# A four-layer graph network: the last row tile as quarters, layer 1's inner units kept as rows, degrees behind a conditional

## The chip, the cores and the metric

The kernel runs on one core of a Trainium2 chip. The metric is the device time of one execution in microseconds (us). Engines: PE (TensorE), DVE (VectorE), ACT (ScalarE), POOL (GpSimd) and SP (SyncE, which here only issues transfers). Every matrix product is in float32; one product in the program is two PE instructions in the trace.

## The reference

A graph of N = 2708 nodes with D = 256 features passes four layers; each adds a graph step and a feed-forward step to x. Layers 0 to 2 are touched.

```python
# layer 0, graph: msg = layernorm(x) @ W + B
#   weights = where(adj < 1, exp(-2 * (1/adj - 1)**2), 0);  x += weights @ msg
# layer 0, feed-forward: 8 experts, each row goes to its best 2
#   h = gelu(xn @ W1[e] + b1[e]);  out += w[e] * (h @ W2[e] + b2[e])
# layer 1, graph
A = adj + jnp.eye(adj.shape[0], dtype=adj.dtype)
D = 1.0 / jnp.sqrt(jnp.sum(A, axis=1))
A = A * D[:, None] * D[None, :]
support = input @ W
out = A @ support                       # relu(out + b)
# layer 1, feed-forward: one hidden layer for all experts, each row goes to its best 1
H = jax.nn.gelu(xf @ W1 + b1, approximate=False)      # 1024 units
probs = jax.nn.softmax((H @ Wg + bg) / TEMP, axis=-1)
assign = jnp.argmax(probs, axis=-1)
for e in range(Wd.shape[0]):
    y = H @ Wd[e] + bd[e]
    sel = (assign == e)[:, None]
    out = out + jnp.where(sel, probs[:, e:e + 1] * y, 0.0)
# layer 2, graph: attention with a mask adj > 0, out = (e @ h) / sum(e)
```

## The kernel before

Rows are cut into 22 tiles of 128 (NT); the last has 20 (LAST; FULL = 21 is its number). x stays in SBUF for the whole program.

**Graph steps.** The adjacency comes transposed from memory. The row tiles of the result are made in groups (GROUPS: 9, 7 and 6 tiles; GROUPS1: 8, 8 and 6; in layer 2 by fives). For a group, the loop `for j in range(NT)` takes one strip `adrow` of 128 source rows (20 in the last), turns it into weights (`weigh` in layer 0: Ln, Exp, Exp on ACT and two DVE steps; in layer 1 a mask, and the identity added on the diagonal; in layer 2 the attention weights `e`) and multiplies it into one accumulator for each tile of the group. These products are lines 739 (layer 0), 965 (layer 1) and 1159 (layer 2). At j = 21 only 20 of the 128 rows that a product can take are there. The last row tile of the result is made apart, with products by columns of 32 (`last_sums`, L256).

**Sending.** When a group is complete, `send` (layer 0) or `send1` (layer 1) normalizes its rows, computes the gate, and `route` gives each row a place in a list ordered by expert; POOL scatters the rows to that place in memory (`taken`), with the row's number and weight behind the 256 features (XW = 258). In layer 1 the gate needs the hidden units H, so `send1` computes them (`hidden`, L317), with the weights `w1`. Send1 of a group is computed among the products of the next one. In layer 0 the buffer `xr` of the last send is that of the send before, whose scatter has to land first (the DVE normalization is L182).

**Blocks.** The feed-forward steps take the list in blocks of 128 places, each with one expert. The class `Blocks` runs items of two blocks: POOL gathers the rows (`xs<-taken`, L465), PE turns them (L518), DVE copies them (L524), PE computes the units (L551) and ACT their gelu (L553), PE makes the output (L560), DVE adds the bias and weighs (L562, L563), and POOL scatters rows to `given` (L451). In layer 0 an item has two blocks of one expert; in layer 1 each block has its own expert, and L551 computes again the units that send1 has had. The first items (NA) hold full blocks of the first groups only, so they can start before the last group is routed. A fixed number (ALWAYS) of the others is always run; what may remain stands under a conditional, `run_rest`, a branch that every engine takes (L569).

**The seam to layer 1.** In the shadow of layer 0's blocks DVE adds up the adjacency's strips into `cs` (128 partial sums for each node). After the last block, but ahead of the conditional, 22 products with a column of ones give the degrees, each copied by DVE (L814, L815). Behind the conditional SP loads `both`, the two results of every row (`given`), which DVE adds to x (L869) before layer 1's normalization and projection (L195, L238; L920 scales by the inverse root of the degree, which DVE makes by Newton steps, L152 to L158).

**Order and memory.** Instructions are issued on each engine in the program's order as a scheduler at build time leaves it. SP's queue has all large loads; POOL has the gathers, the scatters and small loads. Buffers come from pools with a given number of buffers; a load waits until its buffer's last reader is done.

```python
te.matmul(p[:q, n - pair[0], :], lhsT=ad[:, k : k + q],
          rhs=sup[:r, j, :], start=(j == 0 and n == pair[0]),
          stop=(j == NT - 1 and n == pair[-1]))
```

Of the kernel before, what the change touches and what calls it, by code (L numbers as in the profile page):

```python
# [66 lines left out]
def adj_ffn4(ctx: ExitStack, tc: tile.TileContext, a: dict, out: bass.AP):  # L67
# [116 lines left out]

    def shift(st, G):

        nb = small.tile([P, G], F32, name="nb", tag=f"nb{G}", bufs=2)
        v.scalar_tensor_tensor(nb, st[0][:, :, 0], -1.0, st[1], op0=ALU.mult, op1=ALU.mult)
        return nb
# [61 lines left out]
    def last_sums(p, cols, values, n):  # L251
# [10 lines left out]
        return p[:LAST, :n]  # L262

# [210 lines left out]

    class Blocks:
# [4 lines left out]

        def __init__(self, pool, l, each, given, weights):
            self.pool, self.each, self.given = pool, each, given
            self.weights, self.ahead, self.rows, self.at = weights, [], [], [0, 0]
            self.late = None
            self.ik, self.ok = f"taken{l}", f"given{l}"

        def fetch(self, item):

            ei, b = item[0][0], item[1]
            n = 2 * P // self.each  # L490
            es = [nc.values_load(ei[0:1, i : i + 1], engines=[mybir.EngineType.SP], min_val=0,
                                 max_val=E - 1,
                                 skip_runtime_bounds_check_because="at most E - 1 by a minimum")
                  for i in range(n * b, n * b + n)]
            self.ahead.append(self.weights(self.at[0], es))
            self.at[0] += 1

        def fetch_rows(self, item):
            (_, ix, _), b, past, src, full = item
            n = 2 * P // self.each  # L500
# [7 lines left out]
            for k in range(2):  # L508
                i = ix[:, b, k : k + 1] if n == 1 else ix[:, 2 * b + k, :]
                gather(xs[:, k, :], src, i, src.shape[0] - 1, self.ik, past)  # L510
# [16 lines left out]
        def run(self, pool, items, during=None, after=None):  # L527
# [9 lines left out]
            for n in range(len(items)):  # L537
# [20 lines left out]
                for k in range(2):  # L558
                    for f in range(HC):
                        te.matmul(q[:, k, :], lhsT=hT[:, f, k * P : (k + 1) * P], rhs=w2[k][:, f, :],  # L560
                                  start=(f == 0), stop=(f == HC - 1))
                    v.tensor_tensor(y[:, k, :], q[:, k, :], w2[k][:, HC, :], ALU.add)  # L562
# [4 lines left out]
        def run_rest(self, pool, items, left, most):  # L567
# [3 lines left out]
            pin(scattered[self.ok][-1].name)  # L571

# [29 lines left out]
    taken = [tc.dram_tile([2 * N, XW], F32, name="taken0"), tc.dram_tile([N, XW], F32, name="taken1")]  # L602
# [14 lines left out]
    with ExitStack() as l0:  # L617
        hw = l0.enter_context(tc.tile_pool(name="h0", side="right", reuse_waits="tile", bufs=1))

        def weights0(b, es):  # L620
# [3 lines left out]
            i = nc.sync.dma_start(wa, a["L0_ffn_W1b"][bass.ds(es[0], 1)].rearrange("e p n -> p (e n)"))  # L624
# [4 lines left out]
            nc.sync.dma_start(wb, a["L0_ffn_W2p"][bass.ds(es[0], 1)].rearrange("e p n -> p (e n)"))  # L629
            w2 = wb.rearrange("p (f d) -> p f d", d=D)  # L630
            return wa[:, :2048].rearrange("p (c h) -> p c h", c=DC), wa[:, 2048:], (w2, w2)
# [939 lines left out]
```

## Time and profile before

| | us |
|---|---|
| median of 3 runs (lowest to highest) | 2080.28 (2075.45 to 2080.8) |
| the profiled execution | 2077.27 |
| its span, first to last instruction | 2075.3 |
| PE busy | 1974.2 (95%) |
| DVE, ACT, POOL busy | 1098.1, 661.8, 287.4 |

The mean granted clock of PE is 0.967 of full speed; 226.64 MB are moved. By the trace, layer 0's graph step ends at about 262 us, its feed-forward step at 635, the seam to layer 1 lasts to 701 (products begin inside it), layer 1's graph step ends at 982 and its feed-forward step at 1193, layer 2's graph step at about 1458 and its feed-forward step at about 1650; layer 3 takes the rest.

How to read the lines: a group gives line, engine, operation, output<-input by the program's names, shapes and count, then busy time and the mean ns of one, then the idle time of the engine just before and what ended it. Matmuls are pipelined, so their mean duration is longer than the distance from one to the next. A windows row gives the stretch and its length, each engine's busy time with its instructions, the granted clock, the busy share of the 16 DMA engines, and GB/s. A row of waits gives the total, the number and the longest. In the chain and the timeline the first number is the start and the second the length.

### The profile page before, as it was taken

Reading aid. Unit: us, or ns where it says so; the run is one execution under the profiler, and the core shown is the slowest. Engines: PE = TensorE matmul, PEld = TensorE weight load, DVE = VectorE, ACT = ScalarE, POOL = GpSimd, SP = SyncE. Lnnn points to the kernel's source line nnn. Section 1 sums busy time; section 2 is a strip of 40 time slices with the busy share of each in tenths; the row PEclk is TensorE's granted clock in tenths of the full one; section 3 lists DMA queues with packets and bytes.
Section 4 is the critical chain, followed back from the end, with each engine's and each line's share of the span. In section 5 each row is a group of like instructions: output and inputs, shape, how many; then the busy total and the mean of one; then the engine's idle time right before and its main releaser. Section 6 shows DMA issues by size and latency. Waiting matters only on the chain.

```text
span 2075.3 us, 25886 instructions
## 1 busy us (share of the span) xinstructions
PE 1974.2 (95%) x9673; PEld 1422.3 (69%) x9673; DVE 1098.1 (53%) x2513; ACT 661.8 (32%) x1449; POOL 287.4 (14%) x315
## 2 busy tenths in 40 slices
PE   7999979999996999999999979999899999999997
PEld 5888868888885888877788858888566622232334
DVE  7677742543335231334321165455355588897876
ACT  8778722222223204031422251223234410120112
POOL 1004362333320000103133110000000000000000
PEclk9999979999997999999999989999899999999999
DMA  8435557877744341524256330000101000000000
GB/s 266 140 106 147 191 192 266 334 286 295 282 147 134 110 132 43 154 54 147 88 187 210 138 94 1 1 1 1 41 1 31 16 1 21 21 26 11 16 11 24
DMA packets 80611, 226.64 MB, mean 109 GB/s; under 512 B 15218, under 2 KB 38746, under 8 KB 71264
## 3 DMA queue, kind: packets, MB, share of 16 engines
q1 hardware_dynamic: 69056, 196.17, 28.4%
q0 software_dynamic: 11424, 28.74, 4.1%
q8 instruction: 80, 1.31, 0.3%
q14 instruction: 51, 0.42, 0.1%
HBM read 206.46 MB, written 20.65 MB: 109 GB/s over the span
## 4 chain that ended last, share of the span: by engine, by line
PE 55%; DMA 5%; issue 3%; DVE 2%; ACT 2%; POOL 1%; POOLq 0%; DVEq 0%; SPq 0%; ACTq 0%
PE num L1483 11%; PE acc L965 9%; PE ps_acc L1159 9%; PE ps_tmp L317 7%; PE den L1494 6%; DMA given<-ys,xs 4%; PE ps_acc L1335 3%; PE ps_tmp L238 3%; PE ps_tmp L195 1%; PE ps_acc L238 1%; PE ps_tmp L897 1%; POOL xs L465 1%; PE ps_acc L551 1%; POOL given L451 0%; DMA mine<-given 0%
## 5 line engine op out<-in xcount | busy, mean ns | idle before, releaser
L1478 DVE SCALAR_TENSOR_TENSOR e<-arena,G,mask 128x1024 f32<-128x1024 f32 (+2 forms) x264 | 294.2, 1150 | 44.3 <-PE den L1494 43.9
L560 PE MATMUL yacc<-wb,hTs 128*128 128x256 f32 x1152 | 263.1, 381 | 0.9 <-DVE ys L562 0.7
L1483 PE MATMUL num<-e,wh 128*64 128x512 f32 (+4 forms) x1056 | 243.6, 558 | 0.0
L560 PEld LDWEIGHTS yacc<-wb,hTs 128*128 128x128 f32 x1152 | 216.4, 191 | 30.6 <-DVE ys L562 2.3
L965 PE MATMUL acc<-sup,adrow 128*128 128x256 f32 (+1 forms) x924 | 214.4, 390 | 0.0
L739 PE MATMUL acc<-msg,wt 128*128 128x256 f32 (+1 forms) x924 | 208.6, 383 | 0.0
L1159 PE MATMUL ps_acc<-hh,e 128*128 128x257 f32 (+1 forms) x924 | 207.9, 381 | 0.0
L965 PEld LDWEIGHTS acc<-sup,adrow 128*128 128x128 f32 (+1 forms) x924 | 176.7, 195 | 30.6 <-issue 5.5
L739 PEld LDWEIGHTS acc<-msg,wt 128*128 128x128 f32 (+1 forms) x924 | 174.2, 191 | 27.2 <-issue 1.8
L1159 PEld LDWEIGHTS ps_acc<-hh,e 128*128 128x128 f32 (+1 forms) x924 | 171.4, 190 | 28.6 <-issue 2.5
L551 PE MATMUL ps_acc<-xTs,wa 128*128 128x256 f32 x768 | 179.2, 386 | 6.4 <-issue 4.1
L1483 PEld LDWEIGHTS num<-e,wh 128*64 128x64 f32 (+1 forms) x1056 | 74.3, 138 | 155.2 <-issue 121.6
L553 ACT ACTIVATE hTs<-ps_acc,wa 128x256 f32<-128x256 f32 x192 | 90.6, 473 | 257.8 <-PE yacc L560 171.3
L551 PEld LDWEIGHTS ps_acc<-xTs,wa 128*128 128x128 f32 x768 | 142.1, 192 | 35.2 <-issue 4.6
L196 ACT COPY xT<-ps_tmp 128x256 f32<-128x256 f32 x120 | 40.9, 363 | 322.5 <-PE ps_tmp L195 322.2
L1494 PE MATMUL den<-e,wh 128*32 128x512 f32 (+4 forms) x1056 | 137.9, 551 | 0.0
L562 DVE TENSOR_TENSOR ys<-yacc,wb 128x256 f32<-128x256 f32 x72 | 30.5, 424 | 199.7 <-PE yacc L560 199.5
L1156 DVE SCALAR_TENSOR_TENSOR e<-Rb,G,mask 128x640 f32<-128x640 f32 (+2 forms) x110 | 85.2, 775 | 94.3 <-PE ps_acc L1159 94.3
L451 POOL DMA_INDIRECT taken<-xr,r_ix x66 | 78.1, 1183 | 359.7 <-DVE b_vec L387 190.2
L451 POOL DMA_INDIRECT given<-ys,xs x72 | 91.8, 1275 | 208.7 <-DVE ys L563 161.2
L942 DVE TENSOR_SCALAR mask<-adrow 128x1024 uint8<-128x1024 f32 (+1 forms) x66 | 41.5, 629 | 134.4 <-DMA adrow<-in_adjT 134.2
L465 POOL DMA_INDIRECT xs<-taken,b_ix x72 | 75.0, 1042 | 191.0 <-DVE xTs L524 90.6
(392 smaller groups left out, 2464.8 us busy)
## 6 DMA issues: line engine op xcount, KB each, us to landing
adhalf<-in_adjT SPq DMA_DIRECT2D x42, 677.0 KB
wb<-in_L_ffn_W2p SPq DMA_DIRECT2D x24, 1152.0 KB
wb<-in_L_ffn_Wdp SPq DMA_DIRECT2D x24, 1152.0 KB
wa<-in_L_ffn_W1b SPq DMA_DIRECT2D x24, 1028.0 KB
adrow<-in_adjT SPq DMA_DIRECT2D x42, 512.0 KB
adrow<-in_adjT SPq DMA_DIRECT2D x42, 320.0 KB
adrow<-in_adjT SPq DMA_DIRECT2D x21, 576.0 KB
adrow<-in_adjT SPq DMA_DIRECT2D x21, 448.0 KB
```

The source lines that it names most:

```text
L317: te.matmul(p[:, :w], lhsT=w1[:, c, f * P : (f + 1) * P], rhs=xnT[:, c, c0 : c0 + w], start=(c == 0), stop=(c == DC - 1))
L451: i = g.indirect_dma_start(out=dst, out_offset=bass.IndirectOffsetOnAxis(ap=ix, axis=0), in_=src, in_offset=None, bounds_check=bound, oob_ ...
L465: i = g.indirect_dma_start(out=dst, out_offset=None, in_=src, in_offset=bass.IndirectOffsetOnAxis(ap=ix, axis=0), bounds_check=bound, oob_ ...
L551: te.matmul(p[:, f % 2, :], lhsT=w1[:, c, f * P : (f + 1) * P], rhs=xT[:, c, :], start=(c == 0), stop=(c == DC - 1))
L553: s.activation(hT[:, f, :], p[:, f % 2, :], AF.Gelu, bias=bias[:, f : f + 1])
L560: te.matmul(q[:, k, :], lhsT=hT[:, f, k * P : (k + 1) * P], rhs=w2[k][:, f, :], start=(f == 0), stop=(f == HC - 1))
L739: te.matmul(p[:q, n - pair[0], :], lhsT=wt[:, k : k + q], rhs=msg[:r, j, :], start=(j == 0 and n == pair[0]), stop=(j == NT - 1 and n == p ...
L965: te.matmul(p[:q, n - pair[0], :], lhsT=ad[:, k : k + q], rhs=sup[:r, j, :], start=(j == 0 and n == pair[0]), stop=(j == NT - 1 and n == p ...
L1159: te.matmul(p[:q, : D + 1], lhsT=e[:r, k : k + q], rhs=hh[:r, j, :], start=(j == 0), stop=(j == NT - 1))
L1478: v.scalar_tensor_tensor(e[:r, :w], Rb[:r, k, :w], G[:r, j, 2 * pair + k, :], mask[:r, j, c0 : c0 + w], op0=ALU.max, op1=ALU.mult)
L1483: te.matmul(num[k * DK : (k + 1) * DK, hf, :q], lhsT=wh[:r, j, 2 * pair + k, :DK], rhs=e[:r, h0 - c0 : h0 - c0 + q], start=(j == 0), stop= ...
L1494: te.matmul(den[z : z + Q, :q], lhsT=wh[:ri, i, 2 * pair + k, DK : DK + 1].to_broadcast([ri, Q]), rhs=e[:ri, h0 - c0 : h0 - c0 + q], start ...
```

## The change

Four parts are made together.

1. *Row quarters.* At j = 21 the strip's 20 rows are loaded several times, each time at another quarter of 32 partitions, with the columns of other tiles beside them (`last_rows`; POOL sets the tile to ones first). `spread_out` copies the 20 rows of values to all four quarters. `last_product` multiplies with one quarter of the array, at its row position, and `by_turns` orders the tiles so that four in a row differ in quarter and in PSUM tile. In layer 0 this moves to j = 19 of the first group and j = 12 of the others, and the weights need a third of the columns; in layers 1 and 2 it stays last.
2. *Degrees.* The products with ones go behind the conditional, into one PSUM tile with two reads, and Ln and Exp on ACT take the place of the copies and DVE's Newton steps. The additions of `both` to x are ordered behind the last `shift`.
3. *Layer 0's last `xr`* gets a pool of its own.
4. *Layer 1's units as rows.* send1 turns its units back to rows (8 transposes a tile), DVE copies them, and POOL writes them to memory (`hid`). `taken` now has a row number and a weight only. The class `Units` runs single blocks: it gathers the names, gathers by them the rows of `hid` (128 rows of 1024), turns them (8 transposes, two ACT copies), and makes the output as before. Names have one buffer for each block, set to ones once (`MOST` of them), gathered rows three, Wd three. NA is 9 instead of 8, ALWAYS 15 instead of 16. The first names and rows are gathered at j = 17 of the last group, the first Wd after its last product.

```diff
+    def spread_out(values):
+        n = values.shape[1]
+        p = ps_tmp()
+        for z in range(0, P, Q):
+            te.matmul(p[z : z + Q, :n], lhsT=ident[:LAST, :Q], rhs=values[:LAST, :], start=True,
+                      stop=True, tile_position=(0, z))
+        s.copy(values, p[:, :n])
+    def last_rows(dst, parts):
+        g.memset(dst, 1.0)
+        for q, k, c0, w in parts:
+            nc.sync.dma_start(dst[q * Q : q * Q + LAST, k : k + w],
+                              a["adjT"][FULL * P :, c0 : c0 + w])
+    def last_product(p, q, weights, k, values, stop=True):
+        te.matmul(p, lhsT=weights[q * Q : q * Q + LAST, k : k + P],
+                  rhs=values[q * Q : q * Q + LAST, : p.shape[1]], start=False, stop=stop,
+                  tile_position=(q * Q, 0))
+    def by_turns(own):
+        return [(n, t, k) for z in range(2) for n, (t, k, _) in enumerate(own) if n % 2 == z]
...
+    class Units(Blocks):
+            self.names = pool.tile([P, MOST, 2], F32, name="names")
+            g.memset(self.names, 1.0)
+            self.hs = pool.tile([P, 3, HC * P], F32, name="hs")
+            g.memset(self.hs, 0.0)
...
+        def turn(self, pool, h):
+            hT = pool.tile([P, HC, P], F32, name="hTs", bufs=3)
+            for f in range(0, HC, 4):
+                p = ps_acc()
+                for i in range(4):
+                    te.transpose(p[:, i * P : (i + 1) * P], h[:, (f + i) * P : (f + i + 1) * P], ident)
+                s.copy(hT[:, f : f + 4, :], p.rearrange("p (f t) -> p f t", f=4))
+            return hT
...
+        def more(self, weights=True):
+            while self.names_todo and len(self.named) + len(self.rows) < 4:
+                self.fetch_names(self.names_todo.pop(0))
+            while self.rows_todo and len(self.rows) < 3:
+                self.fetch_rows()
+                self.rows_todo -= 1
+            while weights and self.todo and len(self.ahead) < 2:
+                self.fetch(self.todo.pop(0))
...
+                y = pool.tile([P, D], F32, name="ys", bufs=2)
+                q = pools["psum"].tile([P, W], F32, name="yacc", bufs=2)[:, :D]
+                for f in range(HC):
+                    te.matmul(q, lhsT=hT[:, f, :], rhs=w2[:, f, :], start=(f == 0), stop=(f == HC - 1))
+                v.tensor_tensor(y, q, w2[:, HC, :], ALU.add)
+                v.tensor_scalar(y, y, m[:, 1:2], None, op0=ALU.mult)
+                scatter(self.given, m[:, 0:1].bitcast(I32), y, self.given.shape[0] - 1, self.ok)
...
+            xr = (tp if len(parts) == 1 else own_rows[0]).tile(
+                [P, GMAX if len(parts) == 1 else G, 2, XW], F32, name="xr", bufs=1)[:, :G]
...
         work0.run_rest(hc, more, left[0], ALWAYS)
-        for t in range(NT):
-            r = rows(t)
+        for q, t0, t1 in ((P, 0, FULL), (LAST, FULL, NT)):
             d = ps_tmp()
-            te.matmul(d[:r, :1], lhsT=cs[:, t * P : t * P + r], rhs=ones, start=True, stop=True)
-            v.tensor_copy(deg[:r, t : t + 1], d[:r, :1])
+            for t in range(t0, t1):
+                i = te.matmul(d[:q, t : t + 1], lhsT=cs[:, t * P : t * P + q], rhs=ones,
+                              start=(t == t0), stop=(t == t1 - 1))
...
+            lnexp(deg[:q, t0:t1], d[:q, t0:t1], AF.Ln, bias=ones[:q])
+        lnexp(deg, deg, AF.Exp, scale=-0.5)
...
-        v.tensor_scalar(deg, deg, 1.0, None, op0=ALU.add)
-        deg = rsqrt(tp, deg, NT)
...
+                for i, k, r in own:
+                    t, h = tiles[i], gt.tile([P, HC * P], F32, name="hrow", bufs=2)
+                    for f in range(0, HC, 4):
+                        p = ps_tmp()
+                        for z in range(4):
+                            te.transpose(p[:r, z * P : (z + 1) * P], hT[:, f + z, k : k + r], ident)
+                        v.tensor_copy(h[:r, f * P : (f + 4) * P], p[:r, :])
+                    g.dma_start(hid[t * P : t * P + r, :], h[:r])
...
+                if j < FULL:
+                    nc.sync.dma_start(ad, a["adjT"][j * P : j * P + r, c0 : c0 + w])
+                else:
+                    last_rows(ad, [(q, 0, c0, w) for q in range(P // Q)])
...
+                if end and j == NT - 5:
+                    past = list(scattered["taken1"])
+                    work1.begin([(full, b, past, taken[1][:held], True) for b in range(NA)])
```

## The prediction

> **What bounds the kernel now.** I read the page's shares first, then the stages as windows, then the groups that the change touches, kept apart by shape, then the waits of PE, the chain, and POOL's timeline at the end of layer 1's last group.
>
> ```profile
> span 2075.3 us, 25886 instructions
> PE 1974.2 (95%) x9673; PEld 1422.3 (69%) x9673; DVE 1098.1 (53%) x2513; ACT 661.8 (32%) x1449; POOL 287.4 (14%) x315
> ...
> core 0: us, PE busy (x) PEld busy (x) DVE busy (x) ACT busy (x) POOL busy (x), PEclk, DMA share, GB/s
> 0.00:262.00 262.00, 245.34 (x1194) 210.10 (x1194) 197.37 (x441) 200.63 (x243) 58.49 (x72) 0.99 0.56 173
> 635.00:701.00 66.00, 46.14 (x216) 35.94 (x216) 35.79 (x137) 29.51 (x78) 2.93 (x5) 0.82 0.42 134
> 701.00:988.00 287.00, 281.28 (x1414) 235.47 (x1414) 96.85 (x296) 46.59 (x97) 26.84 (x26) 0.97 0.38 112
> 988.00:1193.00 205.00, 202.22 (x994) 169.21 (x994) 43.18 (x137) 62.51 (x133) 46.46 (x47) 0.99 0.45 153
> ```
>
> PE is the bound: 95% of the span, 98% of layer 1's products (701 to 988) and 99% of its feed-forward stage (988 to 1193). So TensorE work taken out there counts in full until something else fills the stage, and DMA, at 153 GB/s, is the next resource. Only the seam of 635 to 701 is loose: PE 70%.
>
> ```profile
> L551 PE MATMUL ps_acc<-xTs,L_ffn_W 128*128 128x256 f32 x384 | 91.5, 388 | 7.3 <-DVE xTs L524 7.3
> L518 PE MATMUL turned<-ident,xs 128*128 128x128 f32 x144 | 23.4, 282 | 0.4 <-DVE xTs L524 0.4
> L524 DVE COPY xTs<-turned 128x512 f32<-128x512 f32 x36 | 23.5, 654 | 46.7 <-PE turned L518 46.7
> L965 PE MATMUL acc<-sup,adrow 20*128 20x256 f32 x42 | 11.4, 425 | 0.0
> L1494 PE MATMUL den<-e,wh 128*32 128x512 f32 x672 | 91.3, 600 | 0.0
> L256 PE MATMUL acc<-msg,wt x44: 374/379/403, 209.7 to 212.6; 128*32 128x256 f32 x42, 20*32 20x256 f32 x2
> ```
>
> Busy times overlap, so I price by pitch. On the chain 32 instructions of 256 columns take 6.94 us, and 16 take 3.47: 0.217 each, and a product is two. Four 128x128 transposes take 0.43: 0.108 each. L965's 42 instructions on 20 rows are the last row tile of one layer: 42 x 0.217 = 9.1 us for 20 rows of 128.
>
> ```profile
> PE ps_tmp L195 <- ACT xn L207: 13.2, 1, 13.2
> PE ps_acc L551 <- DVE xTs L524: 7.3, 4, 5.5
> PE ps_acc L195 <- DVE xr L182: 6.6, 1, 6.6
> ...
> 644.40 2.23 issue
> 647.22 6.15 DMA both<-given
> ...
> 967.64 1.04 POOL L465 DMA_INDIRECT xs<-taken,b_ix  x1 [3.99 <-DMA adrow<-in_adjT]
> 982.53 1.51 POOL L465 DMA_INDIRECT xs<-taken,b_ix  x1 [9.41 <-issue]
> ...
> 352.00:362.00 10.00, 10.00 (x50) 8.71 (x49) 1.73 (x4) 1.78 (x4) 3.10 (x3) 1.00 1.00 411
> 382.00:392.00 10.00, 10.00 (x50) 8.71 (x49) 2.75 (x8) 1.42 (x3) 3.10 (x3) 1.00 0.93 365
> 392.00:402.00 10.00, 10.00 (x50) 8.52 (x49) 6.28 (x8) 3.32 (x7) 2.95 (x2) 1.00 0.94 352
> ```
>
> The first three lines are PE's waits (total, times, longest): the three holes that the change touches. The chain shows SP free only at 646.6 and then the load of `both`. POOL's lines show when a gather could start in layer 1. The last three, from layer 0's feed-forward, show the transfer rate when the DMA engines are nearly full: 352 to 411 GB/s, with PE still at 10.00 of 10.
>
> **Layer 1's inner units kept as rows.** Before, each of 12 items of two blocks turns its rows (4 instructions) and computes the inner units again (32 instructions). Out go 384 x 0.217 = 83.3 and 48 x 0.108 = 5.2, together 88.5 us. In come 8 transposes for each of 24 blocks, 192 x 0.108 = 20.8, and 8 for each of 22 row tiles in send1, 176 x 0.108 = 19.0. Net on PE: **-48.7 us**; 14 of the added 19 fall into the products' stage, which has 6 us of slack in 287 and so grows.
>
> The block now costs PE 8 x 0.108 + 16 x 0.217 = 4.34 us, where half an item was 7.14. Its transfers are 1.18 MB of Wd, 0.52 MB of gathered unit rows and 0.13 MB of result: 1.83 MB. That is 4.46 us at 411 GB/s and 5.21 at 352, so DMA becomes the bound of the stage. At the middle row, 365, it is 5.03: 0.69 over PE, on some 18 blocks (the others lie beside send1's third group and have slack): **+12**. Ends: 0, and 24 x 0.87 = +21. POOL per block issues a names gather, a rows gather and a scatter, 3 x 1.3 us (1.0 and a 0.3 gap in its timeline), 3.9 us, which stays under 5.03.
>
> A new wait stands at the end of group 2. Its last row tile is now loaded as quarters into a tile that POOL first sets to ones, and on POOL that memset is queued behind one names gather after four, three row gathers that wait for names to land, and four more. Before, the first gathers could start at 967.6 (the page's line); twelve at 1.3 us and some 2 us for the landing put the memset at about 985, SP's four loads and their landing at about 989, and the first quarter product at 989.5, where PE arrives at 978.5. Behind it on PE queue the blocks' transposes and send1's, and behind the four loads on SP the first Wd. Before, PE idled 5.5 us there in any case (waiting for xTs). Net **+8**, ends 0 (if the first row gathers land early enough to fill) and +12.
>
> In send1 each pair of tiles puts 16 transposes (1.7 us) through four banks that DVE empties with four copies of 128x512, 0.65 each by L524: 2.6 us. DVE is at a third of this stage, but PE comes back to the banks at once: **+3**, ends 0 and 11 x 0.9 = +10. The 22 writes to `hid` (11.5 MB) lie beside 287 us at 112 GB/s; on POOL, at 0.6 to 0.9 us each by its other plain DMAs, they lie ahead of scatters which come only after the routing. Cover gone, they would cost 7 us a group. Sum of the part: -48.7 + 12 + 8 + 3 = **-26**.
>
> **Row quarters.** Three layers have 42 instructions each, 27.3 us. The trace has no product by rows of 32; the nearest are those by columns of 32: L256 stands at (212.6 - 209.7)/43 = 0.067 an instruction and L1494 at 0.116 with 512 columns. The lower end of the gain is none (0.217 as now); the upper end is four at a time, 7, 6 and 8 rounds in the three layers x 0.433 = 9.1 us, a gain of 18.2. I take 0.116, since here each product loads 128 columns of weights and 16 loads with tiny products (L346) take 1.73, 0.108 each: 126 x 0.116 = 14.6, **-12.7**. Each spreading is four small products and an ACT copy (0.47 by L920's row) with PE behind it: about 1.3 us in layer 0, layer 1 and layer 2, where the second copy has products between: **+4**. The loads grow by 9 DMAs of SP in each of layers 0 and 1; three Wd issues take 2.78 us, so 0.93 each, beside products with four or five buffers in hand: nothing, except in group 2, counted above. ACT and DVE save two thirds of the last tile's weights in layer 0, off the path. Ends of the part: -16 and +6.
>
> The Trainium skill, "TensorEngine Tiling (Array Packing)", Key Properties, speaks against this: a change of tiling mode drains TensorE. It gives no price; from the rows here, an instruction's 0.389 less its pitch 0.217 would be lost at 14 changes, 2.4 us, and the sum would be 2037.5. Its "TensorE: Matmul & The Clock Gate" (Measured speedup vs the span model) has 3.07 times for four row tiles of 512 columns, 27.3 to 8.9, and the sum would be 2029. No row of before shows either.
>
> **Degrees behind the conditional.** Between the last block's product (634.97) and 642.5 stand 44 tiny instructions and 22 DVE copies in turn, 0.43 us a tile; the branch on every engine waits for PE, and SP issues `both` at 646.58, though the last scatter had landed at 640.49. Afterwards SP is held by that landing, the products lie beside the load of `both`, and DVE's Newton chain is two ACT steps. 646.6 - 640.5 = 6 us at most; layer 1's own seam, without degrees, has PE idle 10.5 against 13.2 here, 2.7 us less. Nearer the first, since the load itself is on the chain: **-5**. Ends 0 (the `both` tiles wait for memory that the degree products read) and -8 (with the additions held behind the first shift).
>
> **Layer 0's own rows.** The last send's xr gets its own memory; DVE waited 3.3 us (264.3 to 267.6) for the scatter out of the old one within PE's 6.6: **-3.3**, ends 0 and -6.6.
>
> **Sum.** -26 - 12.7 + 4 - 5 - 3.3 = -43 from the profiled run's 2077.27 (its span 2075.3 and 2 us around it): **2034.5**; I say 2035, since the median of the runs, 2080.28, is 3 above the profiled one. Runs of before lie 2075.45 to 2080.8; 0.3% (6 us) is about what can be told from no change.
>
> **Rivals.** (a) *The gathered rows make the stage transfer-bound at less than the best rate.* For it: in 1060 to 1100 the rate never passed 285 GB/s; 300 would be 6.1 us a block, +32 in place of +12: 2055. Against: demand was only half. (b) *Quarters do not run side by side.* By by_turns the products of one round differ in rows and in PSUM tile, but no row of before shows such a product: 12.7 lost, 2048; with a drain at each change 2050. (c) *Slower: POOL's gather of 4 KB rows.* All indirect DMAs of before move about 1 KB a row at 1.0 us (0.91 to 2.48); none shows whether that time grows with the row. If four times, a block is 1.3 + 4.3 + 1.3 = 6.9 us in POOL's order; without the DMA term the sum is -55, so at 55/18 = 3.05 over PE, a period of 7.4 us, the kernel is no faster, and above it slower: at 8 us, 2088. Against: taken and xs take the same 1.0, as if a price by instruction. (d) *Degrees and xr hidden anyway*, the wait going to the scatter's landing: 8 lost, 2043.
>
> **How the numbers follow.** Forecast, with (d) in it, 0.62: 2013 to 2052. (b) without (a): 0.10. (a): 0.15, 2045 to 2072. (c): 0.13, of which 0.10 slower and 0.03 within 0.3%. Faster is 0.87. The range leaves out (c) and little above it: 2008 to 2070.
>
> **What would show it.** PE products L551 with L_ffn_W gone and PE busy about 60 us less; blocks of the stage at 4.5 to 5.2 us with a DMA share above 0.9; quarter products at about 0.116 us an instruction (0.217 if (b)); `both` issued near 640.5 and the L195 after it near 650; PE idle about 10 us ahead of the quarter product of group 2, released by a load of adrow. The prediction is wrong if rows gathers on POOL last over 2 us, if send1's groups grow by more than 19 us, or if that idle is not there.

## The result and the profile after

The changed kernel takes 2048.13 us (median of 4 runs, 2038.41 to 2048.95) where the kernel before takes 2079.87: a ratio of 0.9841, 95% interval 0.9808 to 0.9874, that is 1.6% or some 33 us faster. The forecast was 2035, so the direction held and the gain was three quarters of the one told. The profiled execution has 2048.93 us, its span is 28.1 us shorter than the one before.

Two lines of the page of the changed kernel: PE has 57.8 us less work, and still 94% of a shorter span.

```profile
span 2047.2 us, 25961 instructions
PE 1916.4 (94%) x9641; PEld 1374.6 (67%) x9641; DVE 1103.8 (54%) x2503; ACT 639.0 (31%) x1407; POOL 333.0 (16%) x369
```

So 58 us of PE's work are gone and 28 us of time. The stages say where the rest went. Each is read from the first or last instruction of PE that marks it, in the two profiled executions:

| stage | before | after | change |
|---|---|---|---|
| layer 0's graph step, to the first transpose of the last send | 268.1 | 262.2 | -5.9 |
| from there to layer 0's last block | 366.9 | 368.6 | +1.7 |
| the seam, to the end of layer 1's projection | 65.9 | 59.6 | -6.3 |
| layer 1's products and sends, to the last product of group 2 | 280.9 | 305.5 | +24.6 |
| from there to layer 1's last block | 211.4 | 171.9 | -39.5 |
| to layer 2's first attention product | 46.6 | 45.5 | -1.1 |
| layer 2's graph step | 214.4 | 212.7 | -1.7 |
| the rest, not touched | 621.1 | 621.2 | +0.1 |

Ten instructions of adjacency products (10 x 0.217 = 2.2 us) that lay inside the projection before lie behind it now; the seam's true gain is 4.1. Layer 1's two rows as windows, first of the kernel before, then of the changed one (length; PE busy; ...; granted clock, DMA share, GB/s at the end):

```profile
700.90:981.80 280.90, 280.44 (x1412) 235.03 (x1412) 90.65 (x277) 46.65 (x97) 22.28 (x22) 0.98 0.37 105
981.80:1193.20 211.40, 203.31 (x998) 169.75 (x998) 49.39 (x157) 62.51 (x133) 51.02 (x50) 0.98 0.46 161
```

```profile
690.40:995.90 305.50, 290.23 (x1558) 244.32 (x1557) 109.80 (x311) 45.41 (x97) 43.66 (x49) 0.98 0.43 123
995.90:1167.80 171.90, 148.03 (x807) 125.60 (x806) 49.94 (x160) 43.71 (x85) 74.95 (x79) 0.92 0.73 257
```

The block stage, which PE filled to 96% before, now leaves PE idle for 23.9 of 171.9 us (8.1 before), and the clock granted there fell from 0.98 to 0.92. PE's waits in the changed kernel from 985 to 1175 show what it idles for (total, times, longest); the first belongs to the row above, ahead of the last quarter products, and stands about where PE waited 5.5 us for `xTs` before:

```profile
PE acc L286 <- DMA adrow<-in_adjT: 7.8, 1, 7.8
PE ps_acc L635 <- DMA hs<-hid,names: 7.3, 2, 6.6
PE ps_acc L635 <- ACT hTs L636: 5.1, 2, 3.2
PE yacc L674 <- DVE ys L675: 3.8, 1, 3.8
PE yacc L674 <- DMA wb<-in_L_ffn_Wdp: 3.8, 2, 2.3
PE ps_acc L635 <- issue: 3.3, 3, 1.1
```

The idle time is not spread over the stage. Windows of 10 us of the changed kernel, three from the middle of the stage and one from its second half:

```profile
1070.00:1080.00 10.00, 3.72 (x16) 2.96 (x16) 1.48 (x4) 0.00 (x0) 7.70 (x8) 0.84 0.82 296
1090.00:1100.00 10.00, 3.37 (x14) 2.28 (x13) 0.78 (x2) 1.61 (x4) 8.47 (x11) 0.70 0.28 72
1100.00:1110.00 10.00, 6.41 (x24) 5.07 (x23) 2.24 (x7) 1.61 (x3) 2.12 (x3) 0.79 0.68 237
1140.00:1150.00 10.00, 10.00 (x56) 8.92 (x55) 1.56 (x4) 2.15 (x4) 5.09 (x6) 1.00 1.01 419
```

In the second half PE is full, a block takes 4.33 us, and the DMA engines deliver 419 GB/s: the transfers do keep up with PE. In two of the three windows from the middle PE works a third of the time and POOL (the fifth figure) is busy for 8 us of 10, and the transfers are down to 72 GB/s in one of them. And the clock is lower in these windows, 0.70 to 0.84, so the products that follow a hole are slow too: PE's timeline has the 16 instructions of a block's output at 3.62 us when the stage runs, and at this after the holes.

```profile
1099.71 5.82 PE L674 MATMUL yacc<-wb,hTs 128*128 128x256 f32 x16
...
1110.23 5.41 PE L674 MATMUL yacc<-wb,hTs 128*128 128x256 f32 x16 [3.83 <-DVE ys L675]
...
1143.37 3.62 PE L674 MATMUL yacc<-wb,hTs 128*128 128x256 f32 x16
```

Low clock does not need a hole, though. In the kernel before it fell to 0.57 among layer 1's products, where PE had not been idle at all:

```profile
766.00:774.00 8.00, 8.00 (x23) 6.00 (x22) 8.00 (x17) 0.00 (x0) 0.00 (x0) 0.57 0.35 115
```

The middle has three holes, each of another kind. The first, 6.57 us up to 1080.55, is the wait for the rows of the first block that needs the last group's routing. Its chain stands in the trace: the routing's products from 1046.64, POOL's last scatter of names issued at 1058.11 and landed at 1064.77, the first names gather at 1065.56, the gather of this block's rows at 1072.27, PE at 1080.55. In the second, from 1091.05 to 1098.80, PE makes four transposes 1.4 us apart with no wait that the profile names, and then waits 3.17 us for ACT's copy. The third, 3.83 us ahead of 1110.23, ends with DVE's `ys`, and DVE had stood still for a weight of layer 2:

```profile
1097.94 0.77 POOL L1210 DMA_DIRECT2D w_l<-in_L_gnn_WT  x1
...
1107.76 0.76 DVE L250 TENSOR_TENSOR o<-w_l,L_gnn_a_r 128x256 f32<-128x256 f32 x2 [9.57 <-DMA w_l<-in_L_gnn_WT]
...
1109.76 0.42 DVE L675 TENSOR_TENSOR ys<-yacc,wb 128x256 f32<-128x256 f32 x1
```

In the kernel before, POOL issues this load at 1201.44, behind the blocks. In the changed one the build-time order puts it and DVE's steps on it among the blocks; `ys` follows these steps on DVE and so waits for the load too. In nine of the twelve kernels with units as rows PE has 0.6 to 3.8 us of such a wait right behind these steps, in one 9.35 (below), and in two none. No run moves the load, so what it costs in time is not shown.

### The profile page after: what moved, and what is told of

It reads as the page before. It is cut to its first block, busy times and chain, and to the rows that moved or that the text cites. A ratio compares the mean times of both kernels' runs of the same rounds, so it can differ in the third digit from the quotient of the medians.

```text
span 2047.2 us, 25961 instructions
## 1 busy us (share of the span) xinstructions
PE 1916.4 (94%) x9641; PEld 1374.6 (67%) x9641; DVE 1103.8 (54%) x2503; ACT 639.0 (31%) x1407; POOL 333.0 (16%) x369
## 4 chain that ended last, share of the span: by engine, by line
PE 55%; issue 5%; DMA 5%; DVE 4%; POOL 3%; ACT 2%; POOLq 0%; SPq 0%; DVEq 0%; ACTq 0%
PE num L1643 11%; PE ps_acc L1319 9%; PE acc L1124 8%; PE ps_tmp L347 7%; PE den L1654 6%; PE ps_acc L1495 3%; PE ps_tmp L241 3%; DMA given<-ys,xs 2%; PE ps_tmp L198 1%; PE ps_acc L241 1%; PE ps_tmp L1045 1%; POOL given L481 1%; POOL names L495 1%; PE yacc L674 1%; DMA adrow<-in_adjT 1%
## 5 line engine op out<-in xcount | busy, mean ns | idle before, releaser
L1124 PE MATMUL acc<-sup,adrow 128*128 128x256 f32 x882 | 200.7, 385 | 2.8 <-DVE o L1076 1.5
L1319 PE MATMUL ps_acc<-hh,e 128*128 128x257 f32 x882 | 199.2, 382 | 2.0 <-ACT o L1264 2.0
L863 PE MATMUL acc<-msg,wt 128*128 128x256 f32 x882 | 198.1, 381 | 2.4 <-DVE x L886 1.2
L1124 PEld LDWEIGHTS acc<-sup,adrow 128*128 128x128 f32 x882 | 166.4, 192 | 31.0 <-issue 4.6
L863 PEld LDWEIGHTS acc<-msg,wt 128*128 128x128 f32 x882 | 165.2, 190 | 28.1 <-DVE wt L824 2.1
L1319 PEld LDWEIGHTS ps_acc<-hh,e 128*128 128x128 f32 x882 | 163.7, 190 | 29.6 <-ACT o L1264 5.0
L587 PE MATMUL yacc<-wb,hTs 128*128 128x256 f32 x768 | 175.5, 381 | 0.5 <-DVE ys L589 0.5
L674 PE MATMUL yacc<-wb,hTs 128*128 128x256 f32 x384 | 94.7, 400 | 7.6 <-DVE ys L675 3.8
L589 DVE TENSOR_TENSOR ys<-yacc,wb 128x256 f32<-128x256 f32 x48 | 20.4, 424 | 134.3 <-PE yacc L587 134.3
L1654 PEld LDWEIGHTS den<-e,wh 128*32 128x32 f32 (+1 forms) x1056 | 30.9, 108 | 90.0 <-issue 86.7
```

What stands on the lines that cost most here:

```text
L674: te.matmul(q, lhsT=hT[:, f, :], rhs=w2[:, f, :], start=(f == 0), stop=(f == HC - 1))
L863: te.matmul(p[:q, n - pair[0], :], lhsT=wt[:, k : k + q], rhs=msg[:r, j, :], start=(j == 0 and n == pair[0]), stop=(j == FULL - 1 and n == ...
L1124: te.matmul(p[:q, n - pair[0], :], lhsT=ad[:, k : k + q], rhs=sup[:r, j, :], start=(j == 0 and n == pair[0]), stop=False)
L1319: te.matmul(p[:, : D + 1], lhsT=e[:, k : k + q], rhs=hh[:, j, :], start=(j == 0), stop=False)
L1654: te.matmul(den[z : z + Q, :q], lhsT=wh[:ri, i, 2 * pair + k, DK : DK + 1].to_broadcast([ri, Q]), rhs=e[:ri, h0 - c0 : h0 - c0 + q], start ...
```

## The experiments

The times need one plain remark first. Executions of one kernel with the units kept as rows lie up to 13 us apart (2030.2 to 2043.2 for one of them below), and the untouched rest behind layer 2's graph step alone differs by 9 us among the profiled executions (616 to 626 us). So a difference of 5 us between two medians decides little here; I read stages beside the times, each from one profiled execution. For layer 1 that is the length from the end of its projection to its last block: 477.4 us in the changed kernel, 494.5 in the kernel before with the ten products counted in.

**The units alone.** In this kernel the quarters (in layers 0, 1 and 2), the degrees behind the conditional and the own xr are undone together. Three pieces of the edit:

```diff
-            for j in range(FULL):
+            for j in range(NT):
...
-            xr = (tp if len(parts) == 1 else own_rows[0]).tile(
+            xr = tp.tile([P, GMAX, 2, XW], F32, name="xr", bufs=1)[:, :G]
...
+            v.tensor_copy(deg[:r, t : t + 1], d[:r, :1])
```

> The changed kernel with the quarters, the degrees behind the conditional and layer 0's own xr all undone: layer 1's units as rows alone. By the prediction's terms for this part, -26: 2051 to 2054. By the stage times of the changed kernel (18 us of its gain lie in the other three parts, read at the end of layer 0's graph step, at the seam and in layer 2): 2064 to 2068, so this part alone would bring 12 to 15 us.

2058.58 us (2053.13 to 2065.22), ratio 0.9908, interval 0.9887 to 0.9929. This part brings some 19 us of time, between the two expectations. Its windows, the same two stretches:

```profile
702.60:999.60 297.00, 295.20 (x1540) 248.74 (x1540) 109.74 (x309) 45.03 (x96) 36.01 (x44) 0.98 0.42 121
999.60:1167.60 168.00, 146.96 (x807) 124.28 (x806) 48.44 (x158) 43.61 (x85) 78.55 (x82) 0.94 0.75 266
```

PE's work grows by 14.8 us in the products' stage, as the 13.9 of the sum had it, and falls by 56.3 in the block stage, where the sum had 88.5 - 20.8 - 5.2 = 62.5. PE idles 21.0 there. Both holes and low clock are there without any quarter, so they come with the units. The other three parts together are worth the difference of the ratios, 0.7%, 14 us, with an uncertainty of some 8.

**The ones of the strips by DVE.**

```diff
     def last_rows(dst, parts):
-        g.memset(dst, 1.0)
+        v.memset(dst, 1.0)
```

> The changed kernel with the ones of the quarters' strips written by DVE and not by POOL. Theory (POOL's order): the memset no longer stands behind nine names gathers and three rows gathers, the four loads of layer 1's last group land before PE arrives, PE's wait of 7.8 us ahead of the first quarter product goes, and the first Wd loads issue about 8 us earlier; some 5 us are left at the end (block 0 still needs rows and Wd): 2043 us. Rival (the loads are late for another reason, such as the buffer they go to): the wait stays at 7 to 8 us and the time at 2048.

2041.97 us (2032.48 to 2044.72), ratio 0.9806 (0.9776 to 0.9836). The cause of the wait is shown. In the changed kernel POOL, SP and PE stood like this at the end of group 2 (timeline: start, length; the last line is the first quarter products):

```profile
987.27 1.01 POOL L495 DMA_INDIRECT names<-taken,b_ix  x1 [0.30 <-issue]
988.59 1.00 POOL L495 DMA_INDIRECT names<-taken,b_ix  x1 [0.30 <-issue]
989.89 1.00 POOL L495 DMA_INDIRECT names<-taken,b_ix  x1 [0.30 <-issue]
990.89 0.65 POOL L280 MEMSET adrow<- 128x640 f32 x1
...
991.56 1.42 SPq L282 DMA_DIRECT2D adrow<-in_adjT  x4
...
993.47 2.45 PE L286 MATMUL acc<-sup,adrow 20*128 20x256 f32 x10 [7.81 <-DMA adrow<-in_adjT]
```

PE's first quarter product followed at 993.47. With the memset on DVE the wait is gone altogether, and the last product of group 2 ends 9 us earlier (986.9 against 995.9). But PE's waits behind it, from 985 to 1166, became these:

```profile
PE ps_acc L635 <- DMA hs<-hid,names: 10.7, 6, 6.9
PE yacc L674 <- DMA wb<-in_L_ffn_Wdp: 7.7, 3, 3.9
PE ps_acc L635 <- ACT hTs L636: 4.3, 2, 2.4
PE yacc L674 <- DVE ys L675: 4.2, 3, 2.6
```

The block stage grew from 171.9 to 178.3, so layer 1 is 3.3 us shorter (474.1), not 8. The time fell by 6, of which only half lies in layer 1; in the profiled executions 3.7 us are in the last part, which the edit does not touch (617.5 against 621.2), and 1.2 in layer 0's graph step, which has quarters too.

**The later names behind the rows.** After the last group's routing POOL issued the names gathers up to four in a row, ahead of the rows of the next blocks.

```diff
-            gather(m, src, ix[:, b, :], src.shape[0] - 1, self.ik, past)
+            i = gather(m, src, ix[:, b, :], src.shape[0] - 1, self.ik, past)
+            if not full and self.got is not None:
+                tc.add_manual_dep(i.ins, self.got.name, ..., reason="order")
```

> The changed kernel with each names gather of the later fifteen blocks ordered behind the rows gather that was issued last, so that POOL no longer issues up to four names in a row. Theory (POOL's order): between the routing of the last group and the middle of the stage POOL is busy without a gap and the rows are late, PE waits some 15 us there for rows, copies and Wd; with names spread out most of the 6.6 us wait for rows and a part of the others goes: 2039 us. Rival (the stage is bound by transfers of 1.83 MB a block, as the prediction had it): the waits only move and the time stays within 2 us of 2048.

2042.3 us (2040.31 to 2048.84), ratio 0.9824 (0.9799 to 0.9848); layer 1 takes 472.7, 4.7 us less. The waits for copies, `ys` and issue shrank to 2.8 in total, but the long wait for rows stayed (6.4), and the waits for rows together grew from 7.3 to 10.4, so POOL's run of names explains the part around that hole and not the hole.

**Both edits, and the full blocks held back.** The second of these kernels orders the transposes of the third and later full blocks behind send1's gate products, too.

```diff
-                    turned = self.turn(pool, self.rows[0][1])
+                    turned = self.turn(pool, self.rows[0][1], gates[-1] if n >= 2 else None)
```

> The changed kernel with the ones written by DVE and the later names gathers behind the rows gathers: the two edits that were each 6 us faster. If they act on different waits (the group's end; the stretch after the routing) they add up: 2036. Rival (what is gained at the group's end is lost again before the rows of the later blocks are there, since that chain starts at the routing): 2040 to 2042.

> The changed kernel with the ones written by DVE, the later names behind the rows (as in the two runs before), and the third and later full blocks kept behind the gate products of the last group's send1, so that PE routes the last rows earlier and has seven full blocks left for the chain that follows, where it had five. Theory (after the full blocks PE waits for the chain routing, scatter, names, rows): at 4.34 us a block two more cover 8.7 us more, the longest wait for rows (6.4 to 6.9 us) goes, and against the two edits without this one the time falls by 3 to 7 us; PE may wait 2 to 3 us more inside send1: 2032 to 2037. Rival (what is late is set by the transfers alone): no change against those two, 2037 to 2040.

Both edits: 2036.16 us (2030.21 to 2043.2), ratio 0.9777 (0.9741 to 0.9812). With the blocks held back: 2038.69 (2032.22 to 2041.87), 0.9786 (0.9763 to 0.9808). Layer 1 takes 466.3 and 462.5. The two edits do add up in layer 1, and more than that (3.3 + 4.7 against 11.1). Holding blocks back shortened it by 3.8 us, and the wait that the theory named is gone: the first block behind the routing waits 6.57 us for its rows in the changed kernel, 1.75 with the two edits and not at all here. But others stand in its place. The longest wait for rows, 5.0, is now at a full block (4.3 with the two edits), and the waits for rows together are still 13.3 us after 15.9. The times do not tell the two apart. Either kernel is faster than both the kernel before and the changed one; their intervals touch the changed one's at most at its end.

**One full block less.**

```diff
-    NA, MOST = 9, (N - E) // P + E + 1
+    NA, MOST = 8, (N - E) // P + E + 1
...
-    ALWAYS = 15
+    ALWAYS = 16
```

> The changed kernel with 8 full blocks that may start before the last group is routed, and 16 later ones, where it has 9 and 15; the blocks are the same in number. Theory (the hole after the full blocks is a wait for the chain routing, scatter, names, rows): one block less to cover it, the longest wait for rows grows by up to 4.3 us from 6.6, time 2051 to 2053. Rival (transfers or POOL's load over the whole stage set the end): the same work, no change, 2048 within the 5 us by which executions differ, and the longest wait stays near 6.6.

One run of 2057.59 us. But layer 1 takes 477.9 us, as in the changed kernel (477.4), and from the routing of the last group to the last block it is 120.6 against 120.9; the time went to layer 0 and to the untouched rest. Behind group 2 PE's two longest waits are 8.3, for which the profile names nothing that ended it, and 7.2, for the rows of the first block behind the routing (6.6 in the changed kernel). A hole that is simply too few blocks for a chain of fixed length would have grown the stage by four; it did not. But the chain has no fixed length: from the routing's first product to the transposes of the first block behind it are 33.9 us in the changed kernel and 27.4 here. So this run speaks neither for the chain nor against it.

**Half of each row.**

```diff
-        hid = tc.dram_tile([N, HC * P], F32, name="hid")
+        hid = tc.dram_tile([N, HC * P // 2], F32, name="hid")
...
-                    g.dma_start(hid[t * P : t * P + r, :], h[:r])
+                    g.dma_start(hid[t * P : t * P + r, :], h[:r, : HC * P // 2])
...
-            g.indirect_dma_start(out=h, out_offset=None, in_=self.hidden[:n, :],
+            g.indirect_dma_start(out=h[:, : HC * P // 2], out_offset=None, in_=self.hidden[:n, :],
```

> The changed kernel in which only the first 512 of the 1024 units are written to memory and gathered; the other half of each block's rows is left as it was set at the start, so half of the inner units are left out of layer 1's output; every instruction stays. A block's transfers fall from 1.83 to 1.57 MB. Theory of the prediction (the stage is bound by transfers at 365 GB/s, 5.03 us a block): 4.34 us a block, some 12 us less between the routing of the last group and the end of layer 1's feed-forward step (120.9 us), with PE's waits for rows and Wd there gone. Rival (POOL's order and the chain from the routing to the rows): 0 to 5 us less, the wait of 6 to 7 us after the full blocks still there.

One run, 2031.87 us, on a chip where the kernel before takes 2069.72; the full rows on that chip are the run with the old xr below (2040.86). From the routing to the last block: 115.8 us, with full rows 116.3 there and 120.9 in the changed kernel's own run. The windows still have the hole, at low transfer rates:

```profile
1065.00:1075.00 10.00, 5.37 (x22) 4.84 (x23) 0.78 (x2) 1.17 (x2) 7.78 (x8) 0.66 0.56 185
1085.00:1095.00 10.00, 2.63 (x6) 2.18 (x7) 4.11 (x12) 0.00 (x0) 5.83 (x7) 0.50 0.56 145
1105.00:1115.00 10.00, 10.00 (x56) 8.92 (x55) 1.56 (x4) 2.15 (x4) 4.78 (x5) 1.00 0.96 369
```

Taking away 0.26 MB of every block's 1.83 changed the stage by half a microsecond on the same chip, where the prediction's theory has 12. But the longest wait here is not one for rows or Wd. It is that for `ys` behind layer 2's weight:

```profile
1089.25 0.76 DVE L250 TENSOR_TENSOR o<-w_l,L_gnn_a_r 128x256 f32<-128x256 f32 x2 [15.22 <-DMA w_l<-in_L_gnn_WT]
...
1092.37 5.94 PE L674 MATMUL yacc<-wb,hTs 128*128 128x256 f32 x16 [9.35 <-DVE ys L675]
```

PE waits 8.0 us for rows and 0.9 for Wd here, 14.8 and 1.7 with full rows on that chip. So fewer bytes may have shortened those waits while this one, 9.35 for 3.14, took the gain. The theory that the whole stage is bound by transfers is refuted; that bytes have no part in the hole is not shown.

**All at one quarter.**

```diff
-    last_product(acc[n // 2][:, n % 2, :], n // 2, ad, k, sup[:, FULL, :],
+    last_product(acc[n // 2][:, n % 2, :], 0, ad, k, sup[:, FULL, :],
...
-    last_product(p[:, : D + 1], n % 4, e, k, hh[:, FULL, :])
+    last_product(p[:, : D + 1], 0, e, k, hh[:, FULL, :])
```

> The changed kernel with all last-tile products of layers 1 and 2 at the first quarter of the rows (the other three quarters hold the same values, so the result is the same). Theory (the gain is that different row quarters work side by side): instructions of these products stand 0.217 us apart and 84 of them cost 84 x (0.217 - 0.08) = 11 us more, some 6 to 11 at the end: 2054 to 2059. Rival (the gain comes from weights of only 20 rows, wherever they stand): the distance stays at 0.06 to 0.11 and the time at 2048.

One run, 2054.07 us, the low end of the theory; layer 1 takes 483.9, 6.5 more, of which 2.4 are a longer wait ahead of group 2's quarter products (10.2 against 7.8). PE's timeline, first of the changed kernel, layer 1's first group and a group of layer 2:

```profile
756.96 1.15 PE L286 MATMUL acc<-sup,adrow 20*128 20x256 f32 x16 [0.59 <-issue]
...
1260.42 1.13 PE L286 MATMUL ps_acc<-hh,e 20*128 20x257 f32 x10
```

then with one quarter (the second line is layer 1's second group):

```profile
759.15 5.54 PE L286 MATMUL acc<-sup,adrow 20*128 20x256 f32 x16 [0.59 <-issue]
...
886.39 3.71 PE L286 MATMUL acc<-sup,adrow 20*128 20x256 f32 x16
...
1269.30 2.43 PE L286 MATMUL ps_acc<-hh,e 20*128 20x257 f32 x10
```

The first instruction of a row starts at its first figure, and the last lasts 0.375, so 16 stand (1.15 - 0.375)/15 = 0.052 us apart in the changed kernel, a quarter of 0.217. At one quarter it is 0.222 in layer 1's second group and 0.228 in layer 2. The 0.344 of the first group is not the quarter's price: there the distance doubles half way, from 0.216 to 0.427, and the clock of 759 to 766 is 0.63. The quarters do work side by side, four at a time. But in group 2 of the changed kernel, behind its wait of 7.81 us, ten instructions took 2.45 us, more than ten common ones at 0.217, so there nothing was gained.

**The degrees ahead of the conditional again.**

```diff
         work0.run_rest(hc, more, left[0], ALWAYS)
-        for q, t0, t1 in ((P, 0, FULL), (LAST, FULL, NT)):
+        for t in range(NT):
...
+            v.tensor_copy(deg[:r, t : t + 1], d[:r, :1])
```

> The changed kernel with the degrees as before: 22 products and copies ahead of the conditional, DVE's Newton steps, no ordering of the additions behind the shifts. By the prediction (-5, at most 6 by the issue of the loads of both): the loads issue 6 us later after the last block's scatter, PE's hole at the seam is 13 instead of 5 us, and the kernel is 4 to 6 us slower: 2052 to 2054. Rival (the seam only moves the wait into layer 1's projection, where the changed kernel has its first products of adjacency 28 us after the first transpose and the kernel before had them after 23): 2048 to 2049.

2051.33 us (2049.91 to 2055.63), ratio 0.9862 (0.9843 to 0.9882), 3 us slower than the changed kernel, which the intervals leave open. The stage is clearer. From layer 0's last block, SP issues `both` after 11.7 us here and 6.0 in the changed kernel, and the first transpose of layer 1 comes after 21.6 and 13.6. Here is its line:

```profile
653.55 0.69 PE L198 MATMUL ps_tmp<-ident,xn 128*128 128x128 f32 x2 [14.12 <-ACT xn L210]
```

and that of the changed kernel:

```profile
644.45 0.69 PE L198 MATMUL ps_tmp<-ident,xn 128*128 128x128 f32 x2 [4.74 <-ACT xn L210]
```

So 8 us are won at the head. But the projection ends after 67.8 and 59.6, or 61.8 with the ten products: 6 us are left. In the nine other kernels with the degrees behind the conditional the projection ends 59.5 to 65.5 us after layer 0's last block, or 61.7 to 67.7 with the ten products, so between none and 6 us of the 8 remain. The chain of the changed kernel shows what takes them: 5.70 us of `both<-given` from 642.03, behind the first additions. The rows of `both` arrive one after the other, and PE follows them.

**The quarters undone, and the old xr.**

```diff
-            xr = (tp if len(parts) == 1 else own_rows[0]).tile(
-                [P, GMAX if len(parts) == 1 else G, 2, XW], F32, name="xr", bufs=1)[:, :G]
+            xr = tp.tile([P, GMAX, 2, XW], F32, name="xr", bufs=1)[:, :G]
```

> The changed kernel with the last row tile as before in layers 0, 1 and 2. By the prediction this part brings 12.7 - 4 us of products and costs 8 at the end of layer 1's group 2, so about 1 net: 2049. By the stage times of the runs so far: layer 0 and layer 2 lose some 4 and 2 us, and layer 1, from the end of its projection to its end, gains 7 to 10 (465 us with units alone against 472 to 475 with units and quarters): 2044 to 2047, so the quarters would cost a little in this kernel.

> The changed kernel with layer 0's last xr in the old buffer. By the prediction (-3.3): PE's hole before the last send of layer 0 is 6 to 6.6 us instead of 3.7, the first transpose there comes at 265 instead of 262.2; the rest stays. Rival (the wait for the scatter is hidden now, behind the additions that wait for the group's end): the hole stays at 3 to 4 us.

Without quarters: 2042.27 us where the kernel before has 2069.72 on that chip, ratio 0.9852 (0.9825 to 0.9879) against 0.9841 with them: no difference that can be told. The expectation's number was for the other chip; as a ratio it said 0.983 to 0.984. In the stages the quarters do bring something in layer 2 (212.7 against 216.1 us) and in layer 0, but in layer 1 PE's wait of 7.6 to 10.2 us ahead of L286 (in every run with quarters and POOL's memset) costs more than they save. Over the whole of layer 1 the quarters as built lose: 473.5 us with them (the run with the old xr) against 461.3 without, on the same chip, and 477.4 in the changed kernel against 467.2 with the units alone, the ten instructions counted in. These are differences of single executions, but both point the same way, and the 466.3 with both edits above is about what layer 1 takes without quarters.

With the old xr, one run of 2040.86 us on the same chip. The hole ahead of layer 0's last send is 7.11 us. The profile puts it down to DVE's statistics, but DVE itself stood still for 3.77 us between these and its write to `xr`, and the profile does not name what ended that:

```profile
266.02 0.41 DVE L182 TENSOR_SCALAR xr<-x,mv,var 128x256 f32<-128x256 f32 x1 [3.77 <-issue]
...
266.57 1.09 PE L198 MATMUL ps_acc<-ident,xr 128*128 128x128 f32 x4 [7.11 <-DVE mv L172]
```

With the old buffer the hole is 6.6 (before), 6.0 (the units alone) and 7.1 us, and DVE waits 2.8 to 3.8 ahead of `xr`; with its own memory the hole is 3.1 to 4.9 in ten kernels, without quarters too (3.1), and DVE does not wait there. So the own xr brings some 3 us, with and without quarters. The quarters act on the other term: the products end at 257.9 to 260.4 with them and at 261.5 to 264.2 without.

## Why the prediction was right or wrong

Right in direction and within the range; the sum was 43 and the profile shows 28 (33 by the ratio). The terms against the stages:

- *Layer 0, quarters and own xr:* -6.2 told (-12.7/3 + 1.3 - 3.3), -5.9 measured, and the parts fit: the hole ahead of the last send went from 6.57 to 3.73 us and the products end 3.0 us earlier (261.49 to 258.47). A spreading costs 1.1 us where 1.3 was told (from 113.20 to 114.32). Layer 0's blocks took 1.7 us more, less than that stage differs among the kernels (360.2 to 371.3).
- *The pitch of a quarter product:* 0.116 was told, on the ground that each loads 128 columns of weights; the runs show 0.052 in full rounds of four and (1.13 - 0.375)/9 = 0.084 in layer 2, where a group of five makes a round of four and a round of one. The upper end of the range (four at a time) is what happened, but for group 2 of layer 1 (2.45 us for ten). Rival (b) is refuted by the run with one quarter. Of the two rules of the Trainium skill that were weighed, the 3.07 times of "TensorE: Matmul & The Clock Gate" (Measured speedup vs the span model) was too low for this case (0.217/0.052 = 4.2 in layer 1), and the drain of "TensorEngine Tiling (Array Packing)" (Key Properties) is small if these steps are it: in layer 2 the step from the last common product to the first quarter product is 0.31 us instead of 0.217, and as much on leaving where nothing else is waited for, so 0.1 us a change where 0.17 was taken.
- *The wait at the end of group 2:* told at 11 us (978.5 to 989.5), net +8, for POOL's memset behind the gathers. It was 7.81, from PE's arrival at 985.65 to 993.47, for that reason, which the run with DVE's memset shows. The whole row of the products' stage, +24.6, is near the +23.5 told (13.9 of transposes, 2.3 of copies, 8 of wait, -2.9 of quarters, 2.2 of shifted products), but partly by luck: PE's work grew by 9.8 where 13.2 was told, and its idle time by 14.8 where 10.3 was told, since PE waited 4.0 us more for `xn` and 1.5 for `o`, which the sum did not have.
- *The quarters in layer 1* were told at -2.9 and +8, about +5; by the two comparisons above they cost 10 to 12 us, of which the memset on DVE wins 3.3 back.
- *The block stage:* this step failed in size. Told: -88.5 + 20.8 + 5.2 + 12 + 0.7 = -49.8; measured -39.5. Two things make the 10 us. PE's idle time grew by 15.8 where 12.7 was told, and for another reason than the one told: the 12 were to come from transfers at 365 GB/s through the whole stage, but the second half runs at 404 to 419 GB/s with PE full at 4.33 us a block, which is the lower end (no cost), and the idle time stands in the middle, with transfers at low rates: the chain from the routing to the rows, which the sum has no term for, a hole for which the trace names no cause, and a load of layer 2 ahead of `ys`. And PE's work fell by 55.3 where 62.5 was told, though the instructions are as counted: the granted clock is 0.92 there and was 0.98, and blocks behind a hole take 5.82 and 5.41 us for 3.62. The sum counted holes by their length and not the slow products that stood behind these.
- *Rivals (a) and (c):* the second half of the stage runs at 404 to 419 GB/s with PE full, so (a) falls; POOL's gather of 4 KB rows takes 1.03 us like one of 8 bytes (1.02), so (c) falls.
- *Degrees:* -5 told, -4.1 in the profile, and from -4.2 to +1.8 against the kernel before in the nine others, since the projection behind it follows the arrival of `both`. *Layer 2:* -2.9 told, -1.7 measured; PE waits there 2.0 us for ACT's reads of its banks, which it did not before.

What stays open is what sets the holes in the middle of the block stage, and by how much each counts. POOL's run of names is a part (4.7 us of layer 1 without it). Layer 2's weight on DVE is a part by the trace, not by a run. The chain from routing to rows makes the first of the three holes by the trace, and with the blocks held back that wait is gone; but other waits for rows took its place, and one full block less changed nothing, so its worth in time is not shown. In all kernels with units as rows but one, 7 to 16 us of waits for rows remain; in that one (degrees ahead) 18 us stood at the copies, Wd and issue instead, so the place of the wait moves. That the clock follows PE's idle time is only what some windows show side by side; no run here varied it by itself, 766 to 774 of the kernel before has low clock without idle time, and over the whole run the granted clock is 0.967 in both kernels.

## What to carry over

Work that is taken off a full engine counts only as far as the engine stays full: ask which queue has to feed it at the new pace, in order, in the first microseconds after a dependency (here the routing), and not only whether the mean rate suffices. Look at the granted clock of a stage beside its idle time: here 7 of the 10 us missing in the block stage are PE's own work grown longer. Look, too, at what the scheduler has moved into the stage from behind it: a load that used to stand after the blocks now stops DVE among them. And before a helper's first step (a memset, a small load) is put on an engine, look at what stands ahead of it on that engine's queue.

## What was not expected of the hardware

Four instructions on different quarters of the rows stand 0.052 us apart on average, the full factor of four, although each brings its own 128 columns of weights, and full ones with weights of 128 rows stand 0.217 apart. The granted clock fell to 0.57 over 8 us in the middle of products without a gap. An indirect gather of 128 rows occupies POOL for 1.02 us with 8 bytes a row and for 1.03 with 4096.
